# The last four chunks of a gathered adjacency: rows written straight to their place

## The chip, the cores and the metric

The kernel runs on one core of a Trainium2 chip. The time is device time in microseconds of one execution, as a median of runs. "Before" is the kernel that was tuned already, "after" the same kernel with one change.

## The reference

The input x has the shape (8, 2048, 128), adj is 2048 x 2048 with some 0.4% of entries that are not zero, its diagonal among them. All is float32. B = 8 batches are stacked side by side, so that a row of 128 nodes times (8 x 128) numbers is a chunk; there are 16 chunks.

```python
# layer 0
res = si[:, :, None] + sj[:, None, :] + relation[None] * w_r + g_b     # relation = adj
agg = einsum('bij,bjd->bid', res, inputs)
x   = layernorm(x + agg @ weight + bias)
# layer 1 (both matrices are adj)
x1  = einsum('bnf,nw->bwf', x, A)
x2  = 2.0 * einsum('bnf,nw->bwf', x1, A) - x
x   = layernorm(x + relu(concat(x, x1, x2, x1, x2) @ Theta1 + bias))
```

So adj is multiplied in three times: once as it is in layer 0, and twice transposed in layer 1, which the kernel does as two hops, the first from u to y, the second from y to the output.

## The kernel before

**Sparse rows.** For a block of columns of adj only the rows with an entry count. The kernel finds them on the chip and writes lists of row numbers. Each of the 16 column chunks of 128 has 7 lists of up to 128 rows: four "T" lists, one for each 32 columns; two, one for each 64 columns; and one for the whole 128. The last three are called "H". A product with adj is then, for each chunk, 7 gathers of rows of the right factor (4 KB each, up to 128 rows, into tile `Y` by an indirect DMA) and matmuls of these with the same rows of adj, 32, 64 or 128 columns wide, that were kept in `rc` (for the hops) and `rct` (for layer 0), and one product with the chunk's own 128 x 128 block, whose block of adj (`rd`) and rows are loaded by SP.

**Dense chunks.** In layer 0 the first ND = 4 chunks are computed with all rows. So they need no entry in `rct`; their rows in `rc` are needed in hop 1, where they come as the 11th to 14th of 16 chunks, and in hop 2.

**Filling rc and rct.** A list of `jobs` fills them. A job is one chunk's T lists (4 gathers) or H lists (3 gathers): `get_job` issues the gathers into a staging place, `keep_job` later multiplies by `has`, which is 0 where a list has no row, on DVE, and writes `rc` and `rct`. The 24 jobs of chunks 4 to 15 gather pieces of 256 numbers from `rr_d`, into four places in `st`. The 8 jobs of the dense chunks gather pieces of 128 numbers from adj by the indices `idr`, each of 128 columns of which 32, 64 or 128 are used, and have one staging place, `trp[:, 2]`. So each of these waits for the DVE instructions of the one before it.

**Stages.** Up to some 150 us adj is read and transposed, x is multiplied by the weight, and chunks 0 and 1 of layer 0 are summed. From 150 to 205 us DVE makes the second set of lists (`lists_end` writes the row numbers `idx` and the piece numbers `idr`, which are row times pieces per row plus `col`) while jobs begin. Chunks 2 and 3 of layer 0 follow, dense. From 261 us the loop over chunks c = 4 to 15 of layer 0 runs: rows of the next chunk (`get_rows`), a `keep_job`, a `get_job`, own rows, `rank9`, the listed rows T and H, `z_add`, `make_u` of an earlier chunk (which writes u_d), the load of x two chunks ahead, and `layernorm`. Hop 1 runs from some 432 us, hop 2 from 625.

**Order.** Every engine runs its queue in order. POOL issues all gathers, SP the loads, ACT the stores of u_d, y_d and the output. Rows go into 12 places of `Y` in turn, so a gather waits until PE has used the twelfth one before it. A scheduler places instructions that have nothing to wait for earlier than the text has them; the four gathers of the first dense job, for one, stand in the list stage.

The lines that the change replaces in the loops of layer 0 and of hop 1:

```python
        if c < 15:
            keep_job()
        if c < 13 or c == 14:
            get_job()
...
            if i == 1 and (k % 2 and k < 12 or k == 12):
                keep_job()
                if k < 12:
                    get_job()
```

All times of instructions stand under line 72 in the profile, a helper that records them; so they are told apart by their tiles.

Of the kernel before, what the change touches and what calls it, by code (L numbers as in the profile page):

```python
# [11 lines left out]
ALU = mybir.AluOpType  # L12
# [6 lines left out]
def kernel(  # L19
# [22 lines left out]
    P = 128  # L42
    B, N, D = x.shape
    NC = N // P
    HB = B // 2
    BD = B * D
    TW = 32
    NT = N // TW
    QT = P // TW
    ND = 4  # L50
# [3 lines left out]
    HC = NT // 2 + NC  # L54
    NI = NT + HC
    PAD = 40000
    W = 3 * P
# [16 lines left out]
    pe, dve, act = Tied(nc.tensor), Tied(nc.vector), Tied(nc.scalar)  # L74
    pool, sp = Tied(nc.gpsimd), Tied(nc.sync)

    y0_d = nc.dram_tensor("y0_d", (N, BD), F32).ap()
    rr_d = [nc.dram_tensor(f"rr_d{c}", (N, 2, P), F32).ap() for c in range(ND, NC)]
# [67 lines left out]
    num = const.tile([P, NC], F32)  # L146
    dve.tensor_copy(num, numi)
    coli = const.tile([P, NI], I32)
    pool.iota(coli[:, 0:NT], pattern=[[1, NC], [0, QT]], base=0, channel_multiplier=0)
    pool.iota(coli[:, NT:NT + 2 * NC], pattern=[[1, NC], [0, 2]], base=0, channel_multiplier=0)  # L150
    pool.iota(coli[:, NT + 2 * NC:], pattern=[[1, NC]], base=0, channel_multiplier=0)
    col = const.tile([P, NI], F32)
    dve.tensor_copy(col, coli)
# [41 lines left out]
    zs = {}  # L195
# [126 lines left out]
    def acc_pair():  # L322
        par[0] ^= 1
        return bank[2 * par[0]:2 * par[0] + 2]
# [143 lines left out]
    def lists_end(part):  # L468
        b = bank[6 + part]
        if part == 0:  # L470
            lo, hi = 0, NT
            for r in range(2):
                pe.matmul(
                    b[64 * r:64 * r + 64, 0:NT], lists, ident[:, 64 * r:64 * r + 64], start=True,
                    stop=True, skip_group_check=True, tile_position=(0, 64 * r),
                )
        else:
            lo, hi = NT, NI
            for r in range(2):
                pe.matmul(  # L480
                    b[64 * r:64 * r + 64, 0:HC], lists2[0:2 * HC],
                    ident[0:2 * HC, r * HC:(r + 1) * HC], start=True, stop=True,
                    skip_group_check=True, tile_position=(0, 64 * r),
                )
        pl = b[:, 0:hi - lo]
        s = slice(lo, hi)
        rown = small.tile([P, NT], F32, name=f"rown{part}", tag="rown")[:, 0:hi - lo]
        dve.tensor_scalar(has[:, s], pl, 0.0, None, op0=ALU.is_gt)
        dve.tensor_scalar(rown, pl, 0.0, float(PAD + 1), op0=ALU.is_equal, op1=ALU.mult)
        dve.scalar_tensor_tensor(rown, pl, -1.0, rown, op0=ALU.add, op1=ALU.add)  # L490
        dve.tensor_copy(idx[:, s], rown)
        dve.scalar_tensor_tensor(rown, rown, float(NC), col[:, s], op0=ALU.mult, op1=ALU.add)
        dve.tensor_copy(idr[:, s], rown)
        if part:
            dve.tensor_reduce(miss[:, 2:3], has, AX.X, ALU.add)
            dve.tensor_sub(miss[:, 0:1], miss[:, 0:1], miss[:, 1:2])
            dve.tensor_sub(miss[:, 0:1], miss[:, 0:1], miss[:, 2:3])

    def overflow():
# [3 lines left out]
            b[0:1, 0:1], miss[:, 0:1], ones[:, 0:1], start=True, stop=True, skip_group_check=True,  # L503
        )
        dve.tensor_scalar(over, b[0:1, 0:1], 0.5, None, op0=ALU.is_gt)

    adj128 = adj.rearrange("n (c f) -> (n c) f", f=P)

    def gather(to, src, ids, n, rows):
        pool.indirect_dma_start(  # L510
            out=to, out_offset=None, in_=src,
            in_offset=bass.IndirectOffsetOnAxis(ap=ids[:, n:n + 1], axis=0),
            bounds_check=rows - 1, oob_is_err=False,
        )
# [6 lines left out]
    def strided(t, n, step, w):  # L521
        return t[:, 0:n * step].rearrange("p (n s) -> p n s", s=step)[:, :, 0:w]

    jobs = [("T", c) for c in T_ORDER] + [("H", c) for c in range(ND, NC)]
    for c in range(ND):
        jobs += [("T", c), ("H", c)]
    got, kept = [0], [0]
    last = trp[:, 2].rearrange("p i f -> p (i f)")

    def staged(k):  # L530
        return st[:, k % 4 * BD:] if jobs[k][1] >= ND else last

    def get_job():
        what, c = jobs[got[0]]
        s = staged(got[0])
        got[0] += 1
        for n, i in enumerate(columns(c, what)):
            if c >= ND:
                gather(
                    s[:, n * 2 * P:(n + 1) * 2 * P], rr_d[c - ND].rearrange("n m f -> n (m f)"), idx,  # L540
                    i, N,
                )
            else:
                gather(s[:, n * P:(n + 1) * P], adj128, idr, i, N * NC)

    def keep_job():
        what, c = jobs[kept[0]]
        s = staged(kept[0])
        kept[0] += 1
        m = 2 if c >= ND else 1  # L550
        hc = has[:, columns(c, what)[0]:columns(c, what)[0] + QT]
        for k in range(m):
            if m == 1 or k == 1:
                to = rc[:, c * W:(c + 1) * W]
            else:
                to = rct[:, (c - ND) * W:(c - ND + 1) * W]
            of = s[:, k * P:]
            if what == "T":
                if m == 2:
                    dve.tensor_mul(  # L560
                        to[:, 0:P].rearrange("p (t f) -> p t f", t=QT),
                        strided(of, QT, m * P + TW, TW), hc[:, :, None].to_broadcast([P, QT, TW]),
                    )
                    continue
                for t in range(QT):
                    at = t * (P + TW)
                    dve.tensor_scalar(
                        to[:, TW * t:TW * t + TW], of[:, at:at + TW], hc[:, t:t + 1], None,
                        op0=ALU.mult,
                    )  # L570
                continue
            step = m * P + 64
            dve.tensor_mul(
                to[:, P:2 * P].rearrange("p (t f) -> p t f", t=2), strided(of, 2, step, 64),
                hc[:, 0:2, None].to_broadcast([P, 2, 64]),
            )
            i = NT + 2 * NC + c
            dve.tensor_scalar(
                to[:, 2 * P:3 * P], of[:, 2 * m * P:2 * m * P + P], has[:, i:i + 1], None,
                op0=ALU.mult,  # L580
            )

    def make_ub():
        cs = [trp[:, h].rearrange("p i f -> p (i f)") for h in range(2)]
# [42 lines left out]
    def layernorm(z, name):  # L627
        s = small.tile([P, 4, B], F32, name=f"s_{name}", tag="s")
        dve.tensor_reduce(s[:, 0], z, AX.X, ALU.add)
        dve.tensor_scalar(s[:, 1], s[:, 0], 1.0 / D, None, op0=ALU.mult)  # L630
        dve.tensor_sub(z, z, s[:, 1][:, :, None].to_broadcast([P, B, D]))
        for h in range(2):
            hs_ = slice(h * HB, (h + 1) * HB)
            sq = small.tile([P, HB, D], F32, name=f"sq_{name}_{h}", tag="sq", bufs=1)
            act.activation(sq, z[:, hs_, :], AF.Square)
            dve.tensor_reduce(s[:, 2, hs_], sq, AX.X, ALU.add)
        act.activation(s[:, 3], s[:, 2], AF.Sqrt, bias=epst, scale=1.0 / D)
        rs = small.tile([P, B], F32, name=f"rs_{name}", tag="rs")
        dve.reciprocal(rs, s[:, 3])
        dve.tensor_mul(z, z, rs[:, :, None].to_broadcast([P, B, D]))  # L640

    atx = at4.rearrange("p c (k b f) -> p (c k) b f", k=2, b=B)
    x1t = [atx[:, c] for c in range(8)] + [Y[:, c] for c in range(4, 8)]
# [195 lines left out]
    for c in range(ND, NC):  # L839
        if c > ND:  # L840
            if c > ND + 1:
                get_rows(0, c, "T", y0_d)
            get_rows(0, c, "H", y0_d)
        if c < 15:
            keep_job()
        if c < 13 or c == 14:
            get_job()
        accs = acc_pair()
        own_rows(0, c, accs, True)
        if c + 2 < NC:  # L850
            own0(c + 2)
        rank9(c, accs)
        if c + 1 < NC:
            si_t(c + 1)
        listed(0, c, accs, "T")
        listed(0, c, accs, "H")
        z_add(accs, zs[c])
        for n in [c - 2] if c < 14 else [12, 13] if c == 14 else [14]:
            make_u(n, zs[n], x1t[n], u_of[n])
        if c + 2 < NC:  # L860
            load_z(c + 2)
        layernorm(zs[c], f"0_{c}")


    def hop(i, src, order, there, between):
# [51 lines left out]
        for k, c in enumerate(order):  # L917
            rows(k, "H")
            if k > 1:
                begin(k)  # L920
            fetch(k + 2)
            if k > 0:
                rows(k + 1, "T")
            if i == 1 and (k % 2 and k < 12 or k == 12):
                keep_job()
                if k < 12:
                    get_job()
            listed(i, c, accs[k], "H")
            end(c, accs[k])

# [1 line left out]
        1, u_d, list(range(ND, 14)) + list(range(ND)) + [14, 15], range(12, NC),  # L932
        lambda: make_u(NC - 1, zs[NC - 1], x1t[NC - 1], u_of[NC - 1]),
    )
    assert kept[0] == len(jobs)
    homes[4:9] = homes[9:14]
    hop(
        2, y_d, list(range(9, 14)) + list(range(ND)) + [14, 15] + list(range(4, 9)),
# [96 lines left out]
```

## Time and profile before

| what | value |
|---|---|
| median of 3 runs | 808.93 us (806.57 to 810.0) |
| the profiled execution | 818.08 us, its span 816.3 us, mean granted clock 0.971 |
| busy: PE, DVE, ACT, POOL | 732.8, 394.7, 192.7, 445.2 us |
| gathers of Y from y0_d and y_d ("y_d" in the profile) | 196, mean 1081 ns on POOL |
| gathers of Y from u_d | 112, mean 999 ns |
| gathers into st from rr_d | 84, mean 1075 ns |
| gathers of adj into trp | 28, mean 1010 ns, 5.8 us from issue to landing |

The profile is of one execution. POOL's time of a gather is what it takes to issue it; the transfer follows on the DMA engines. "Idle before" in a timeline is how long the engine had been idle before an instruction, and what ended that. The DMA share of a window is the mean busy share of 16 DMA engines, and GB/s what they moved. A waiting PE is later charged to what landed last.

### The profile page before, as it was taken

Reading aid. Unit: us, or ns where it says so; the run is one execution under the profiler, and the core shown is the slowest. Engines: PE = TensorE matmul, PEld = TensorE weight load, DVE = VectorE, ACT = ScalarE, POOL = GpSimd, SP = SyncE. Lnnn points to the kernel's source line nnn. Section 1 sums busy time; section 2 is a strip of 40 time slices with the busy share of each in tenths; the row PEclk is TensorE's granted clock in tenths of the full one; section 3 lists DMA queues with packets and bytes.
Section 4 is the critical chain, followed back from the end, with each engine's and each line's share of the span. In section 5 each row is a group of like instructions: output and inputs, shape, how many; then the busy total and the mean of one; then the engine's idle time right before and its main releaser. Section 6 shows DMA issues by size and latency. Waiting matters only on the chain.

```text
span 816.3 us, 10067 instructions
## 1 busy us (share of the span) xinstructions
PE 732.8 (90%) x3554; PEld 364.9 (45%) x3554; DVE 394.7 (48%) x591; ACT 192.7 (24%) x439; POOL 445.2 (55%) x432
## 2 busy tenths in 40 slices
PE   4999999997999998988798888898899999999992
PEld 4666566642644343434345243333344454444441
DVE  4664876578341655555533000000100377777775
ACT  3757554321200332313222000000000011111101
POOL 1000000477747876776344677776774777776740
PEclk9999999997999999999899899999999999999997
DMA  8999999999326799999969799899999799999982
GB/s 264 296 314 316 352 292 295 314 398 347 119 89 223 244 346 368 341 344 367 356 224 344 246 364 360 314 365 346 339 372 357 252 343 357 370 385 389 363 299 68
DMA packets 165299, 253.90 MB, mean 311 GB/s; under 512 B 17255, under 2 KB 118020, under 8 KB 163192
## 3 DMA queue, kind: packets, MB, share of 16 engines
q0 software_dynamic: 49280, 146.52, 49.7%
q1 hardware_dynamic: 93200, 81.01, 31.1%
q10 hardware_dynamic: 22760, 25.63, 8.9%
q8 instruction: 30, 0.49, 0.2%
q14 instruction: 29, 0.24, 0.1%
HBM read 234.82 MB, written 58.72 MB: 360 GB/s over the span
## 4 chain that ended last, share of the span: by engine, by line
PE 52%; DMA 29%; issue 6%; ACT 6%; DVE 3%; POOL 2%; ACTq 0%; POOLq 0%; SPq 0%; DVEq 0%
PE bank L72 52%; DMA Y<-u_d,idx 12%; DMA Y<-y_d,idx 8%; DMA st<-rr_d,idx 2%; DMA rd<-rr_d 2%; ACT Y L72 2%; DMA ring<-in_x_dram 2%; POOL Y L72 1%; ACT rct L72 1%; ACT trp L72 1%; DMA trp<-in_adj_dram,idr 1%; DVE s L72 1%; DVE ring L72 1%; ACT at L72 1%; DVE st L72 1%
## 5 line engine op out<-in xcount | busy, mean ns | idle before, releaser
L72 POOL DMA_INDIRECT Y<-y_d,idx x196 | 212.0, 1081 | 93.2 <-PE bank L72 38.0
L72 PE MATMUL bank<-Y,rc 128*32 128x512 f32 (+2 forms) x896 | 219.7, 618 | 21.3 <-DMA Y<-u_d,idx 19.1
L72 POOL DMA_INDIRECT st<-rr_d,idx x84 | 90.3, 1075 | 183.5 <-DVE rown L72 148.3
L72 POOL DMA_INDIRECT Y<-u_d,idx x112 | 111.8, 999 | 53.9 <-issue 29.9
L72 PEld LDWEIGHTS bank<-Y,rc 128*32 128x32 f32 (+2 forms) x896 | 58.6, 130 | 179.3 <-issue 99.5
L72 PE MATMUL bank<-Y,at 128*128 128x512 f32 x256 | 115.2, 601 | 0.0
L72 PE MATMUL bank<-Y,rct 128*32 128x512 f32 (+2 forms) x336 | 77.3, 625 | 8.5 <-DMA Y<-y_d,idx 8.5
L72 DVE TENSOR_REDUCE s<-sq 128x4 f32<-128x512 f32 x64 | 43.9, 686 | 58.0 <-ACT sq L72 58.0
L72 PEld LDWEIGHTS bank<-Y,at 128*128 128x128 f32 x256 | 47.8, 193 | 53.6 <-issue 53.4
L72 DVE COPY ring<-bank 128x512 f32<-128x512 f32 x10 | 6.9, 692 | 110.1 <-PE bank L72 110.1
L72 ACT ACTIVATE sq<-ring 128x512 f32<-128x512 f32 x44 | 27.7, 630 | 129.5 <-DVE ring L72 109.7
L72 PE MATMUL bank<-ring,rd 128*128 128x512 f32 x108 | 51.5, 599 | 5.7 <-DMA rd<-rr_d 4.1
L72 PE MATMUL bank<-ident,rc 128*128 128x128 f32 (+2 forms) x302 | 45.0, 297 | 12.6 <-DMA rc<-in_adj_dram 6.6
L72 PE MATMUL bank<-th,at 128*128 128x128 f32 x384 | 49.2, 283 | 1.9 <-ACT at L72 1.9
L72 PEld LDWEIGHTS bank<-th,at 128*128 128x128 f32 x384 | 46.8, 197 | 6.7 <-ACT at L72 3.8
L72 DVE TENSOR_TENSOR ring<-bank,ring 128x512 f32<-128x512 f32 x26 | 17.3, 688 | 66.0 <-PE bank L72 60.8
L72 DVE TENSOR_REDUCE st<-rc 128x64 f32<-128x2048 f32 x16 | 36.5, 2283 | 25.7 <-DMA rc<-in_adj_dram 25.7
L72 ACT COPY ring<-bank 128x512 f32<-128x512 f32 x34 | 19.9, 586 | 122.5 <-PE bank L72 112.9
L72 PEld LDWEIGHTS bank<-Y,rct 128*32 128x32 f32 (+2 forms) x336 | 20.8, 130 | 57.3 <-issue 32.4
L72 PEld LDWEIGHTS bank<-ident,rc 128*128 128x128 f32 (+2 forms) x302 | 33.8, 150 | 25.5 <-issue 9.1
L72 PE MATMUL bank<-wx,trp 128*128 128x130 f32 x256 | 36.9, 288 | 4.3 <-ACT trp L72 2.2
L72 PE MATMUL bank<-ident,ring 128*128 128x128 f32 x232 | 32.5, 282 | 6.4 <-DMA ring<-in_x_dram 2.8
(142 smaller groups left out, 789.1 us busy)
## 6 DMA issues: line engine op xcount, KB each, us to landing
rc<-in_adj_dram SPq DMA_DIRECT2D x16, 1024.0 KB, 10.9
ring<-in_x_dram SPq DMA_DIRECT2D x25, 512.0 KB, 8.5
rr_d<-in_adj_dram SPq DMA_DIRECT2D x12, 1024.0 KB, 10.8
rr_d<-Y SPq DMA_DIRECT2D x8, 1024.0 KB, 9.0
y_d<-Y SPq DMA_DIRECT2D x16, 512.0 KB, 10.6
u_d<-ring ACTq DMA_DIRECT2D x12, 512.0 KB, 7.0
ring<-y_d SPq DMA_DIRECT2D x11, 512.0 KB, 23.2
ring<-u_d SPq DMA_DIRECT2D x10, 512.0 KB, 3.9
```

Source lines behind the costliest of these rows:

```text
L72: return lambda *a, **k: tc.keep_in_program_order(f(*a, **k))
```

## The change

The dense chunks have no jobs any more. Their 28 gathers write straight into `rc`, each piece just as wide as its list's columns (32, 64 or 128 numbers), so `idr` counts pieces of that width. A gather leaves rows without an entry untouched; so `rc` of a dense chunk is first set to zero, by a comparison "below 0" of a number that the layernorm of chunk 8, 11, 12 or 14 has just computed and that is never below 0. Of the gathers 22 are written in the loop of layer 0 at chunks 10 to 15, and 6 in hop 1, one for each of its first chunks. The tile `trp[:, 2]` is no longer used for staging, and the 24 DVE instructions that masked the dense rows are gone.

```diff
-    pool.iota(coli[:, 0:NT], pattern=[[1, NC], [0, QT]], base=0, channel_multiplier=0)
-    pool.iota(coli[:, NT:NT + 2 * NC], pattern=[[1, NC], [0, 2]], base=0, channel_multiplier=0)
+    pool.iota(coli[:, 0:NT], pattern=[[1, NT]], base=0, channel_multiplier=0)
+    pool.iota(coli[:, NT:NT + 2 * NC], pattern=[[1, 2 * NC]], base=0, channel_multiplier=0)
...
-        dve.scalar_tensor_tensor(rown, rown, float(NC), col[:, s], op0=ALU.mult, op1=ALU.add)
+        for a, z, m in ((0, 32, 32), (32, HC, NC)) if part else ((0, NT, NT),):
+            dve.scalar_tensor_tensor(
+                rown[:, a:z], rown[:, a:z], float(m), col[:, lo + a:lo + z], op0=ALU.mult,
+                op1=ALU.add,
+            )
...
-    for c in range(ND):
-        jobs += [("T", c), ("H", c)]
...
+    direct = []
+    for c in range(ND):
+        direct += [(c * W + t * TW, TW, QT * c + t) for t in range(QT)]
+        direct += [(c * W + P + t * 64, 64, NT + 2 * c + t) for t in range(2)]
+        direct += [(c * W + 2 * P, P, NT + 2 * NC + c)]
+
+    def clear(c, rs):
+
+        dve.tensor_scalar(
+            rc[:, c * W:(c + 1) * W], rs[:, 0:1].to_broadcast([P, W]), 0.0, None, op0=ALU.is_lt
+        )
+
+    def get_direct(n):
+        for at, w, i in direct[:n]:
+            gather(
+                rc[:, at:at + w], adj.rearrange("n (c f) -> (n c) f", f=w), idr, i, N * (N // w)
+            )
+        del direct[:n]
...
-        if c < 15:
+        if kept[0] < len(jobs):
             keep_job()
-        if c < 13 or c == 14:
+        if got[0] < len(jobs):
             get_job()
+        get_direct({10: 2, 11: 3, 12: 4, 13: 4, 14: 5, 15: 4}.get(c, 0))
...
-        layernorm(zs[c], f"0_{c}")
+        rs = layernorm(zs[c], f"0_{c}")
+        if c in (8, 11, 12, 14):
+            clear((8, 11, 12, 14).index(c), rs)
...
-            if i == 1 and (k % 2 and k < 12 or k == 12):
-                keep_job()
-                if k < 12:
-                    get_job()
+            if i == 1:
+                get_direct(1)
```

`layernorm` now returns `rs`, the reciprocal of the standard deviation.

More of the change, by code (lines that the diff above doesn't have):

```diff
@@ L505, in overflow @@
         dve.tensor_scalar(over, b[0:1, 0:1], 0.5, None, op0=ALU.is_gt)
-    adj128 = adj.rearrange("n (c f) -> (n c) f", f=P)
     def gather(to, src, ids, n, rows):
@@ L524 @@
     jobs = [("T", c) for c in T_ORDER] + [("H", c) for c in range(ND, NC)]
-    for c in range(ND):
-        jobs += [("T", c), ("H", c)]
     got, kept = [0], [0]
-    last = trp[:, 2].rearrange("p i f -> p (i f)")
     def staged(k):
-        return st[:, k % 4 * BD:] if jobs[k][1] >= ND else last
+        return st[:, k % 4 * BD:]
     def get_job():
@@ L537, in get_job @@
         for n, i in enumerate(columns(c, what)):
[L538 to L544, printed above, removed]
+            gather(
+                s[:, n * 2 * P:(n + 1) * 2 * P], rr_d[c - ND].rearrange("n m f -> n (m f)"), idx, i,
+                N,
+            )
     def keep_job():
@@ L549, in keep_job @@
         kept[0] += 1
-        m = 2 if c >= ND else 1
         hc = has[:, columns(c, what)[0]:columns(c, what)[0] + QT]
[L552 to L556, printed above, removed]
+        for k in range(2):
+            to = rc[:, c * W:(c + 1) * W] if k else rct[:, (c - ND) * W:(c - ND + 1) * W]
             of = s[:, k * P:]
             if what == "T":
[L559 to L570, printed above, removed]
+                dve.tensor_mul(
+                    to[:, 0:P].rearrange("p (t f) -> p t f", t=QT), strided(of, QT, 2 * P + TW, TW),
+                    hc[:, :, None].to_broadcast([P, QT, TW]),
+                )
                 continue
-            step = m * P + 64
             dve.tensor_mul(
-                to[:, P:2 * P].rearrange("p (t f) -> p t f", t=2), strided(of, 2, step, 64),
+                to[:, P:2 * P].rearrange("p (t f) -> p t f", t=2), strided(of, 2, 2 * P + 64, 64),
                 hc[:, 0:2, None].to_broadcast([P, 2, 64]),
@@ L578, in keep_job @@
             dve.tensor_scalar(
-                to[:, 2 * P:3 * P], of[:, 2 * m * P:2 * m * P + P], has[:, i:i + 1], None,
-                op0=ALU.mult,
-            )
+                to[:, 2 * P:3 * P], of[:, 4 * P:5 * P], has[:, i:i + 1], None, op0=ALU.mult
+            )
+    direct = []
[6 more added lines that the diff above has]
+            rc[:, c * W:(c + 1) * W], rs[:, 0:1].to_broadcast([P, W]), 0.0, None, op0=ALU.is_lt
+        )
+    def get_direct(n):
+        for at, w, i in direct[:n]:
+            gather(
+                rc[:, at:at + w], adj.rearrange("n (c f) -> (n c) f", f=w), idr, i, N * (N // w)
+            )
+        del direct[:n]
     def make_ub():
@@ L640, in layernorm @@
         dve.tensor_mul(z, z, rs[:, :, None].to_broadcast([P, B, D]))
+        return rs
     atx = at4.rearrange("p c (k b f) -> p (c k) b f", k=2, b=B)
@@ L934 @@
     )
-    assert kept[0] == len(jobs)
+    assert kept[0] == len(jobs) and not direct
     homes[4:9] = homes[9:14]
```

## The prediction

> **What bounds the kernel now.** I read the chain of work that ended last first, then the windows by stage, then the timelines of POOL, PE and SP in the two stages that the change touches.
>
> ```profile
> PE 52%; DMA 29%; issue 6%; ACT 6%; DVE 3%; POOL 2%; ACTq 0%; POOLq 0%; SPq 0%; DVEq 0%
> PE bank L72 52%; DMA Y<-u_d,idx 12%; DMA Y<-y_d,idx 8%; DMA st<-rr_d,idx 2%; DMA rd<-rr_d 2%; ACT Y L72 2%; DMA ring<-in_x_dram 2%; POOL Y L72 1%; ACT rct L72 1%; ACT trp L72 1%; DMA trp<-in_adj_dram,idr 1%; DVE s L72 1%; DVE ring L72 1%; ACT at L72 1%; DVE st L72 1%
> ```
>
> Half of the chain is matmul; the largest other piece, 12%, is gathers of u_d, that is hop 1. The windows (columns as in their heading) show what that stage lacks.
>
> ```profile
> core 0: us, PE busy (x) PEld busy (x) DVE busy (x) ACT busy (x) POOL busy (x), PEclk, DMA share, GB/s
> 340.00:376.00 36.00, 33.44 (x168) 14.96 (x165) 20.98 (x35) 11.70 (x24) 27.19 (x28) 1.00 0.99 344
> 376.00:410.00 34.00, 26.72 (x121) 11.33 (x120) 15.55 (x30) 8.13 (x16) 13.85 (x14) 0.90 1.00 363
> 447.00:613.00 166.00, 146.81 (x649) 58.82 (x645) 13.17 (x34) 8.21 (x14) 120.28 (x122) 0.95 0.93 337
> 590.00:613.00 23.00, 21.84 (x103) 9.07 (x103) 1.39 (x2) 1.17 (x2) 16.54 (x18) 0.93 1.00 373
> ```
>
> In 447 to 613 POOL issues 122 gathers, each 0.99 us and then 0.30 us of issue: one per 1.295 us, 158 us of the 166. In 590 to 613, where none of them is a small gather of adj, the transfers run at 373 GB/s; over the whole stage at 337. So hop 1 is bound by POOL's issue rate, with transfers close behind. The reason stands in POOL's timeline:
>
> ```profile
> 456.49 0.99 POOL L72 DMA_INDIRECT Y<-u_d,idx  x1 [0.30 <-issue]
> 460.76 1.00 POOL L72 DMA_INDIRECT trp<-in_adj_dram,idr  x1 [3.29 <-DVE rc L72]
> 462.06 1.00 POOL L72 DMA_INDIRECT trp<-in_adj_dram,idr  x1 [0.30 <-issue]
> 463.37 0.99 POOL L72 DMA_INDIRECT trp<-in_adj_dram,idr  x1 [0.30 <-issue]
> 464.67 0.99 POOL L72 DMA_INDIRECT Y<-u_d,idx  x1 [0.30 <-issue]
> ```
>
> A 64 KB gather of adj holds POOL as long as a 512 KB gather of Y, and the first of a group also waits 3.29 us for DVE to empty the one staging place. PE's floor in hop 1 is lower: the begin of a chunk stands at 596.49 and of the next at 605.63 when nothing is missing, 9.14 us, against a mean of (614.77 - 463.18)/13 = 11.7 us.
>
> In layer 0 PE waits too, but not always for POOL:
>
> ```profile
> 363.36 3.85 PE L72 MATMUL bank<-Y,rct 128*64 128x512 f32 x10 [1.44 <-DMA Y<-y_d,idx]
> 377.33 3.84 PE L72 MATMUL bank<-Y,rct 128*64 128x512 f32 x10 [1.10 <-DMA Y<-y_d,idx]
> 402.08 2.49 PE L72 MATMUL bank<-ring,rd 128*128 128x512 f32 x4 [4.07 <-DMA rd<-rr_d]
> 382.54 1.18 SPq L72 DMA_DIRECT2D rd<-rr_d  x1
> 410.68 0.99 POOL L72 DMA_INDIRECT Y<-y_d,idx  x1 [10.61 <-PE bank L72]
> 425.39 0.99 POOL L72 DMA_INDIRECT Y<-u_d,idx  x1 [6.88 <-issue]
> ```
>
> In chunks 11 and 12 it waits for gathers, POOL being busy without a break until 376. In chunk 14 it waits for its own block, issued on SP at 382.54 and landed at 402.08. POOL by then has gaps (4.46 us before 391.32, 10.61 before 410.68, 6.88 before 425.39; some 23 us with smaller ones).
>
> **The change, part by part.** The instruction order of the two built programs tells where the 28 gathers of adj stand. Before: 4 in the list stage (172.96 to 178), 4 at 412 to 417, 20 between the u_d gathers from 460.76 on. After: 2 ahead of chunk 11's rows, 3 ahead of chunk 12's, 16 between there and the first u_d gather, 7 among the first ten u_d gathers and before the H rows of hop 1. None is later.
>
> *Hop 1.* 20 gathers and the wait go from 447 to 613: 20 x 1.295 + 3.0 = 29 us of POOL, which would leave 137 us. Transfers are next. The stage moved 337 x 166 = 55.9 MB, of which the 20 small ones were at most 20 x 64 KB = 1.3 MB; 54.6 MB at the 373 GB/s of the stretch without them is 146 us, at 360 GB/s 152. I take 151, since gathers will still be held by buffers now and then: -15 us (-29 if POOL alone ruled, -6 if only the transfer time of the 20 goes: their packets at the mean of the ACT queue q10, whose 8.9% of 16 engines' span are 1162 us for 22760 packets, 0.05 us, are 128 x 0.05/16 = 0.4 us each). PE's floor, 9.14 us a chunk, lies below all of these.
>
> *Layer 0, POOL.* The 5 gathers ahead of the rows of chunks 11 and 12 delay these by 2.6 and 6.5 us, and both chunks already wait: up to 6.5 us. Later ones, 16 - 4 = 12 more, 15.6 us, fit into the 23 us of gaps, since rows of chunks 13 to 15 lie some 6, 10 and 20 us ahead of PE. The delay is not all kept: chunk 13 waits 1.64 us and chunk 14 4.07 us for loads whose issue follows the own rows of two chunks earlier (about 30 us from those to landing). With PE 6.5 us late, chunk 13's wait goes (4.9 left), and chunk 14's load, shifted by chunk 11's 2.6, leaves about 2.5 us. After the 4.07 us gap the four own matmuls took 2.49 us instead of 1.88, the rows 7.33 instead of 5.71, at a granted clock of 0.78 in 395 to 410; a shorter gap may save some of that. Against it stands transfer time: the share is 1.00 there, and 12 more small gathers at 0.4 us are 5 us. I take +3 (-2 to +9).
>
> *Start of hop 1.* 7 gathers stand among the first u_d gathers. Two push T rows of the first chunks by 1.3 us each; five fall into the gap before 447.43, where POOL waited 6.85 us for the last u_d to land. They take 6.5 us, so without that cover they would cost 6.5; I take +1.
>
> *DVE.* The 24 masking instructions of the dense chunks go (16 x 0.24, 4 x 0.29, 4 x 0.285, 5 us): nothing, DVE is busy 13 of 166 us in hop 1, and the one POOL wait for them is counted. Four clears of 128x384 come: no such row; between 0.28 (128x128) and 0.69 us (128x512), nearer to the latter, 0.55 each. They follow layernorms 8, 11, 12 and 14, ahead of gaps of 2 to 5 us: nothing; at worst 2.2. One instruction is added to the second list step, on DVE's chain near 192.6: +0.2.
>
> *List stage.* 4 gathers leave POOL at 173 to 178. Nothing: POOL then stops 8.79 us before 234.74 for DVE, and that gap only grows.
>
> *Clears as a wait.* A small gather at the head of POOL's queue now waits for a layernorm, with the next rows behind it. Layernorms 11, 12 and 14 end at 375.95, 390.58 and 426.66; with shifts of 2.6 and 4.9 us in the first two and 0.55 us for the clear that is 379, 396 and, plus the last shift, 427. POOL reaches the places at about 373.3 + 9.1 = 382, after 400, and at 428 plus the last shift. Margins of 3, 4 and 1 us: nothing, but the last is thin, and u_d gathers queue behind it.
>
> Sum: -15 + 3 + 1 + 0.2, about -11. The profiled execution took 818.08 us, 1.8 more than its span of 816.3; it would take 807. It lay 9.15 above the median of 808.93, so the median goes to 798.
>
> **A rule weighed.** The change makes pieces of 512 bytes into pieces of 128 (16 gathers) and 256 (8). The row nearest to a small packet is the ACT queue's 0.05 us at 1.1 KB, which as a bound gives the 0.4 us above. The Trainium skill, "DMA: Bandwidth & Descriptors", Specifications, says that below 512 bytes a transfer loses line rate since it becomes a read-modify-write: a rule against this change. If that doubled a packet, the 12 extra gathers would cost 10 us instead of 5, and the sum would be -6. No run shown so far settles it.
>
> **Rivals.**
> *Gain hidden.* Hop 1 keeps its DMA-bound time (share 0.93: 154 busy us, less 6 for the small ones, with the same holes), so it gives 8, and layer 0 pays the whole 6.5. For it: the share is above 0.9 throughout. Against: 373 GB/s in 590 to 613 with POOL at full pace. Time: 818 - 8 + 8, no change, 807.
> *All of POOL's time.* Hop 1 gains 24 and layer 0 pays nothing, its later waits eating the delay: 808.9 - 23 = 786. Against: a chunk moves 4 MB (7 gathers of some 0.43 MB, by the 35.7 MB and 70 gathers of hop 2's window 640 to 740 at 357 GB/s less 0.59 MB a chunk of other loads and stores; own rows and store of 0.52 MB each), 10.8 us at 373 GB/s and not 9.1.
> *Slower: small packets in the full stage.* From 340 to 410 the transfers have no room. If a 128- or 256-byte packet took as long as a 4 KB one in the saturated stretch (4096 B at 373/16 GB/s, 0.18 us), a gather would cost 1.4 us, the 17 extra ones 24 us ahead of hop 1, and chunks 12 to 15 would wait for own loads; hop 1 gives 15: 809 + 9 = 818. It decides from about 0.11 us a packet on (17 x 128 x 0.11/16 = 15). Against: the 0.05 us row.
> *Not what it says.* The gathers could be moved early, as 4 were before; the instruction order excludes it.
>
> **How the numbers follow.** Forecast 0.58 (798, itself 791 to 804), hidden 0.18 (804 to 811), all 0.12 (784 to 791), slower 0.12 (811 to 822). The range from 787 to 809 leaves out the ends. Differences within 0.5% (4 us, 804.9 to 813.0) count as none, about what a measurement of this kernel can tell. Faster: 0.58 + 0.12 + a little of hidden = 0.72; same 0.16; slower 0.12.
>
> **What would show it.** Right: no adj gather after the H rows of hop 1 begin; 102 gathers of u_d there in about 150 us at above 360 GB/s; chunk 12's wait for gathers up by 4 us, chunk 14's wait for its load down. Wrong: the stage from the first H row of hop 1 shorter by less than 8 us; PE waiting over 5 us in chunk 14 or 15; POOL waiting for DVE at one of the clears, with u_d rows behind.

## The result: 0.4% slower, and where the time went

The changed kernel takes 813.93 us (median; 811.64 to 816.64), beside 809.93 us (806.57 to 817.54) for the kernel before: a ratio of 1.0038, 95% interval 1.002 to 1.0056. The forecast was 798 us.

The chain of work that ended last, in the profile of the changed kernel:

```profile
PE 48%; DMA 32%; issue 6%; ACT 6%; DVE 3%; POOL 3%; ACTq 0%; POOLq 0%; DVEq 0%
PE bank L72 48%; DMA Y<-u_d,idx 15%; DMA Y<-y_d,idx 13%; DMA st<-rr_d,idx 3%; ACT Y L72 2%; POOL Y L72 2%; DMA ring<-in_x_dram 1%; ACT rct L72 1%; ACT trp L72 1%; DVE lists L72 1%; ACT at L72 1%; DVE s L72 1%; DVE st L72 1%; DVE ring L72 1%; DMA gb<-in_L_gnn_g_b_dram 1%
```

The gathers of y_d, which are layer 0's here (and later hop 2's), have gone from 8% to 13% of it. The windows of the changed kernel show the two stages:

```profile
core 0: us, PE busy (x) PEld busy (x) DVE busy (x) ACT busy (x) POOL busy (x), PEclk, DMA share, GB/s
340.00:376.00 36.00, 32.57 (x152) 14.32 (x153) 19.11 (x32) 11.05 (x23) 27.80 (x27) 1.00 0.89 303
376.00:410.00 34.00, 28.53 (x136) 11.62 (x134) 17.25 (x30) 7.99 (x17) 25.12 (x26) 0.90 0.93 323
447.00:613.00 166.00, 153.37 (x706) 65.52 (x706) 10.37 (x15) 9.40 (x17) 108.75 (x111) 0.98 0.96 356
590.00:613.00 23.00, 22.50 (x109) 10.07 (x108) 1.38 (x2) 1.17 (x2) 15.38 (x17) 1.00 0.98 362
```

In hop 1 POOL has idle time now, 111 gathers in place of 122, and the transfers move 356 GB/s. From 376 to 410 it is the other way round: POOL is busy 25.12 of 34 us where it was busy 13.85 before (21.00 in before_a, told next), and the transfers fell from 363 to 323 GB/s (from 340 to 376, from 344 to 303). Another execution of the kernel before (called before_a below), 10 us shorter than the one that the prediction read, has this window:

```profile
447.00:613.00 166.00, 150.65 (x688) 62.40 (x688) 13.86 (x35) 8.79 (x15) 123.38 (x125) 0.99 0.96 351
```

351 GB/s at a share of 0.96, and not 337 at 0.93. So hop 1 had less to win than it seemed: 351 to 356.

Three marks tell the stages apart in every profile: the own rows of hop 1's first chunk ("k0") on PE, its first 64-wide listed matmul ("H", the one behind the last u_d), and the group of 16 theta matmuls with which hop 2 begins. The rows below the fourth are of experiments told further down. All are in us from the start of the span; "hop 1" is the last mark less H. These are profiles from chips on which the kernel before takes 810 to 811 us.

| profile | chunk 12 | 13 | 14 | 15 | k0 | H | theta of hop 2 | hop 1 |
|---|---|---|---|---|---|---|---|---|
| before, as predicted from | 370.20 | 385.97 | 402.08 | 420.91 | 434.27 | 451.66 | 625.16 | 173.5 |
| before_a | 368.87 | 382.55 | 396.42 | 412.01 | 425.38 | 446.80 | 616.58 | 169.8 |
| before_b | 368.21 | 382.09 | 395.63 | 411.95 | 425.38 | 446.19 | 617.66 | 171.5 |
| after | 371.69 | 392.41 | 404.22 | 423.05 | 436.41 | 458.25 | 620.37 | 162.1 |
| none | 370.06 | 383.95 | 397.03 | 412.54 | 425.90 | 447.38 | 612.09 | 164.7 |
| first5_c | 372.74 | 389.98 | 401.78 | 417.30 | 430.67 | 451.90 | 618.28 | 166.4 |
| not_first_c | 370.83 | 384.86 | 399.86 | 417.69 | 431.23 | 457.14 | 618.93 | 161.8 |
| late_c | 369.28 | 382.88 | 396.28 | 411.80 | 425.16 | 449.63 | 616.34 | 166.7 |
| gap | 370.82 | 384.50 | 396.90 | 412.42 | 425.79 | 447.51 | 615.38 | 167.9 |
| gap2 | 369.37 | 383.78 | 398.90 | 417.73 | 431.09 | 452.51 | 615.30 | 162.8 |
| no_own_c | 373.95 | 392.36 | 404.17 | 424.90 | 438.27 | 459.64 | 611.86 | 152.2 |

Against the mean of before_a and before_b, the changed kernel reaches H 11.8 us later, runs hop 1 in 8.5 us less (162.1 against 170.6), and so begins hop 2 3.3 us later; hop 2 takes as long as before (190.1 us from the mark to the end of the span, beside 189.9). That fits the 4.0 us between the medians. The marks are of single executions, which differ by 1 to 2 us: chunk 12, for one, stands at 368.21 to 370.83 in the versions without gathers of adj among the rows of chunks 11 and 12.

Where do the 11.8 us come from? POOL's timeline of the changed kernel, with lines left out:

```profile
376.02 1.00 POOL L72 DMA_INDIRECT rc<-in_adj_dram,idr  x1 [0.30 <-DMA Y<-y_d,idx]
...
382.47 0.98 POOL L72 DMA_INDIRECT Y<-y_d,idx  x1 [1.54 <-DMA Y<-y_d,idx]
...
391.56 1.00 POOL L72 DMA_INDIRECT rc<-in_adj_dram,idr  x1 [0.30 <-issue]
...
421.03 0.99 POOL L72 DMA_INDIRECT Y<-y_d,idx  x1 [0.30 <-issue]
...
430.13 1.00 POOL L72 DMA_INDIRECT Y<-u_d,idx  x1 [4.20 <-PE bank L72]
```

Between 340 and 430 POOL issues every 1.3 us, with two gaps only. The line at 421.03 is the last gather of layer 0, a row of chunk 15. In before_a, where the gaps are, the same gather stands at 406.98:

```profile
387.82 1.33 POOL L72 DMA_INDIRECT Y<-y_d,idx  x1 [2.19 <-PE bank L72]
...
401.77 1.00 POOL L72 DMA_INDIRECT Y<-y_d,idx  x1 [2.75 <-PE bank L72]
...
406.98 1.00 POOL L72 DMA_INDIRECT Y<-y_d,idx  x1 [0.31 <-issue]
...
420.19 0.99 POOL L72 DMA_INDIRECT Y<-u_d,idx  x1 [10.91 <-PE bank L72]
...
442.55 0.99 POOL L72 DMA_INDIRECT Y<-u_d,idx  x1 [6.79 <-DMA u_d<-st]
```

From 340 to that last row before_a has eight gaps of 0.48 us or more, 8.9 us together, which is 6.5 beyond the usual 0.30 us of issue. Its two large gaps, 10.91 and 6.79 us, lie behind the row. The changed kernel puts 18 gathers of adj ahead of it, where before_a has three: 15 more, 15 x 1.295 = 19.4 us. The gaps can take 6.5 of them, 12.9 are left, and the row is 14.05 us later. The lead that POOL had over PE covers a part; PE waits for the rest:

```profile
381.77 7.64 PE L72 MATMUL bank<-Y,rct 128*32 128x512 f32 x22 [4.93 <-DMA Y<-y_d,idx]
411.47 1.93 PE L72 MATMUL bank<-Y,rct 128*64 128x512 f32 x6 [1.10 <-DMA Y<-y_d,idx]
```

The first is in chunk 12, the second in chunk 14. By chunks the lag of after behind before_a is 2.8 us at chunk 12, 9.9 at 13, 7.8 at 14, 11.0 at 15 and 11.0 at k0: chunk 12 loses 7, chunk 13 wins 2 back, chunk 14 loses 3. The wait of 4.93 us is not all of chunk 12's loss: the 22 matmuls behind it took 7.64 us, where all 28 of chunk 13 took 5.71 at a granted clock of 1.00 (395.51 us). From 382 to 388 us the granted clock was 0.68, and by these numbers it cost some 3 us (an estimate).

### The profile page after: what moved, and what is told of

It is laid out like the page before. It is cut to its first block, busy times and chain, and to the rows that moved or that the text cites. A ratio compares the mean times of both kernels' runs of the same rounds, so it can differ in the third digit from the quotient of the medians.

```text
span 810.5 us, 10025 instructions
## 1 busy us (share of the span) xinstructions
PE 730.5 (90%) x3554; PEld 363.8 (45%) x3554; DVE 391.5 (48%) x572; ACT 192.2 (24%) x439; POOL 446.0 (55%) x432
## 2 busy tenths in 40 slices
DMA packets 165299, 252.96 MB, mean 312 GB/s; under 512 B 17256, under 2 KB 118333, under 8 KB 163192
## 4 chain that ended last, share of the span: by engine, by line
PE 48%; DMA 32%; issue 6%; ACT 6%; DVE 3%; POOL 3%; ACTq 0%; POOLq 0%; DVEq 0%
PE bank L72 48%; DMA Y<-u_d,idx 15%; DMA Y<-y_d,idx 13%; DMA st<-rr_d,idx 3%; ACT Y L72 2%; POOL Y L72 2%; DMA ring<-in_x_dram 1%; ACT rct L72 1%; ACT trp L72 1%; DVE lists L72 1%; ACT at L72 1%; DVE s L72 1%; DVE st L72 1%; DVE ring L72 1%; DMA gb<-in_L_gnn_g_b_dram 1%
## 5 line engine op out<-in xcount | busy, mean ns | idle before, releaser
L72 PE MATMUL bank<-Y,rc 128*32 128x512 f32 (+2 forms) x896 | 216.3, 612 | 17.1 <-DMA Y<-u_d,idx 14.6
L72 PE MATMUL bank<-Y,rct 128*32 128x512 f32 (+2 forms) x336 | 80.9, 619 | 15.2 <-DMA Y<-y_d,idx 15.2
L72 ACT COPY Y<-bank 128x256 f32<-128x256 f32 (+1 forms) x72 | 27.8, 397 | 44.0 <-PE bank L72 43.7
```

The costliest lines, as they stand in the source:

```text
L72: return lambda *a, **k: tc.keep_in_program_order(f(*a, **k))
```

## The experiments

The ratio is always to the kernel before on the same chip. The first comparison, the fourth and the fifth were on chips on which the kernel before takes 811 us. The second and the third fell on two other chips, on which it takes 849 and 850 us, at a lower clock and with pauses in layer 0 that the first ones do not have; of these, called the slower chips, the ratios are told, and no stage of theirs is compared with another chip's.

**The kernel before, twice more (before_a, before_b).** No edit.

> The kernel before, unchanged, for a second profile: the first was taken in an execution of 818.08 us, 8 above the median of 22 runs (809.93). Theory Q (POOL's queue: the moved gathers stand ahead of layer 0 rows for which POOL has no slack in a usual run): a usual execution of 808 to 811 us in which chunk 14 does not wait 4 us for its own block, the low clock of 395 to 410 us is missing, and the first H matmul of hop 1 stands at 442 to 446 us instead of 451.66, so that layer 0 really got 12 to 16 us later and hop 1 got 11 us shorter. Theory P (small packets of 128 and 256 bytes load the DMA engines in layer 0): the same here. Theory U (the profile of before was usual up to hop 1, and the 8 us lie elsewhere): first H matmul again at 451 to 452 us, and the difference in hop 1 or hop 2.

> The kernel before, a third profile. Q and P: 806 to 812 us, first H matmul of hop 1 at 442 to 446 us; U: 451 to 452.

808.29 and 809.26 us. Both reach k0 at 425.38 us, 8.9 us earlier than the profile of the prediction, and run hop 1 2 to 3.7 us faster. In that profile PE had waited 4.07 us for an own block in chunk 14, at a clock of 0.78; here the only such waits are 1.84 us in chunk 14 of before_a and 0.56 us in chunk 15 of before_b.

**Without the 28 gathers (none).**

```diff
-        for at, w, i in direct[:n]:
-            gather(...)
         del direct[:n]
```

> The kernel after without the 28 gathers of adj for the dense chunks (their rows in rc stay zero, so their part of layer 1 is left out); clears and all else stay. It is the floor for every placement of the 28. Q: the 21 that stand ahead of hop 1 cost up to 21 x 1.3 = 27 us there, less what gaps cover: 797 to 803 us. P: the packets alone cost the difference to before, 795 to 803. If neither holds (the loss comes from the clears or from the staging place being gone): 810 to 814.

802.47 us, ratio 0.9865 (0.9814 to 0.9916). Beside the changed kernel's 1.0038 that is 14 us, the cost of all 28 gathers where the change has them. Against the kernel before the whole removal gains 11 us (4 us either way), and hop 1 becomes only 5.9 us shorter (170.6 to 164.7). The profiles show 6 of the 11, since before_a and before_b lie 2 to 3 us below their chip's median of 811.12; where the rest is they do not tell. Its window of hop 1, columns as above:

```profile
447.00:613.00 166.00, 157.78 (x705) 65.24 (x706) 11.04 (x16) 9.36 (x16) 105.66 (x107) 0.98 0.97 358
```

With not one gather of adj left the transfers stand at 0.97 and 358 GB/s. The forecast's 151 us for 166, 15 less, was more than there was to be had.

**The same gathers with their rows out of range (oob).**

```diff
-        for a, z, m in ((0, 32, 32), (32, HC, NC)) if part else ((0, NT, NT),):
+        for a, z, m in ((0, 32, 8192), (32, HC, 8192)) if part else ((0, NT, 8192),):
```

> The kernel after with the pieces' row numbers multiplied by 8192 for 64, 32 and 16, so that nearly all rows of the 28 gathers lie out of range and move nothing: POOL issues the same gathers at the same places, and the packets are gone (the dense chunks' part of layer 1 is left out). Q: 811 to 815 us, as after, since POOL's issue is what costs. P: 797 to 804, near the kernel without the gathers.

815.41 us, ratio 1.0043 (1.0017 to 1.0069), as the changed kernel; H at 458.82 us, hop 1 of 163.0. The counts of the trace, first of the changed kernel, then of this one:

```profile
DMA packets 165299, 252.96 MB, mean 312 GB/s; under 512 B 17256, under 2 KB 118333, under 8 KB 163192
```

```profile
DMA packets 165299, 252.36 MB, mean 311 GB/s; under 512 B 17693, under 2 KB 118455, under 8 KB 163192
```

0.60 MB are gone, yet the number of packets is the same. The kernel before, and none, for comparison:

```profile
DMA packets 165299, 253.90 MB, mean 311 GB/s; under 512 B 17255, under 2 KB 118020, under 8 KB 163192
```

```profile
DMA packets 164401, 252.32 MB, mean 315 GB/s; under 512 B 16798, under 2 KB 117559, under 8 KB 162296
```

none has 898 fewer, 896 of them on POOL's queue, which is 32 for each of the 28 gathers. So a gather of 128 pieces shows as 32 packets, and it keeps them when nearly all of its rows are out of range. The bytes of the small pieces show no price, and the loss of layer 0 stays without them. That a packet as such costs nothing is not shown by this run, though it was meant to; what speaks on it is that the versions below keep the same pieces, in other places, and no longer show the loss.

**Seven behind the rows of chunk 15, seven behind the ninth u_d gather, fourteen in hop 1 (late, late_b, late_c).** The clears move with them; those in hop 1 read a number of the y that its chunk has just made, times 0.

```diff
-        get_direct({10: 2, 11: 3, 12: 4, 13: 4, 14: 5, 15: 4}.get(c, 0))
+        get_direct({15: 7}.get(c, 0))
...
-        if c in (8, 11, 12, 14):
-            clear((8, 11, 12, 14).index(c), rs)
+        if c in {13: 0, 15: 1}:
+            clear({13: 0, 15: 1}[c], rs)
...
-                get_direct(1)
+                get_direct({0: 7, 3: 2, 4: 2, 5: 2, 6: 2, 7: 2, 8: 2, 9: 2}.get(k, 0))
...
+            if i == 1 and k in {2: 2, 5: 3}:
+                clear({2: 2, 5: 3}[k], flat(homes[c])[:, BD - 1:BD])
```

> The gathers written straight to rc, but none ahead of any row of layer 0: 7 behind the last rows of chunk 15, where POOL stands still some 10 us for u_d, 7 after the 9th gather of u_d, where it stands still some 7 us for the last u_d, and 14 in hop 1, two for each of seven chunks, held there by clears that read results of hop 1. Theory Q (POOL's issue, charged where POOL has no slack): layer 0 as before, first H matmul of hop 1 at 446 to 449 us, hop 1 shorter by 2 to 6 us than before, together 804 to 809 us where before has 810. Theory Z (writing straight to rc, the clears or the missing staging cost by themselves): first H matmul later than 452, no gain.

0.989 (0.9844 to 0.9937), on the first of the slower chips. Repeated on the other:

> The version with 7 of the 28 gathers behind the rows of chunk 15, 7 behind the ninth u_d gather and 14 in hop 1, two per chunk from its fourth on, again. Theory (placement decides): ratio 0.985 to 0.993, first matmul of hop 1 within 5 us of the kernel before, hop 1 shorter by at least 4 us. Rival (its earlier gain was the other chip's): 0.997 to 1.006, as the changed kernel.

0.9832 (0.977 to 0.9893). And on a chip like the first:

> The version with 7 of the 28 gathers behind the rows of chunk 15, 7 behind the ninth u_d gather and 14 in hop 1, a third time, for a chip on which the kernel before takes about 810 us. Theory (placement decides): ratio 0.985 to 0.993 there, that is 798 to 804 us; first matmul of hop 1 at 446 to 452 us, hop 1 of 162 to 166 us. Rival (the gain was that of a chip on which the kernel before takes 849 us): above 0.997.

808.35 us, ratio 0.9965 (0.9943 to 0.9987). So it is below both kernels, all three times; the size is 0.35% on the last chip and 1.1 and 1.7% on the slower ones, and why it is larger there is open. On the last chip the ratio lies outside of the expected 0.985 to 0.993. POOL's timeline shows the place:

```profile
403.20 0.99 POOL L72 DMA_INDIRECT Y<-y_d,idx  x1 [0.30 <-PE bank L72]
...
420.02 1.00 POOL L72 DMA_INDIRECT Y<-u_d,idx  x1 [5.87 <-PE bank L72]
```

The last row of layer 0 is issued at 403.20, the seven gathers of adj take the time behind it, and the first u_d gather still waits 5.87 us for a place in `Y`. k0 stands at 425.16, as in the kernel before.

**Seven behind layer 0's rows, 21 in hop 1 in groups of four and three (straight).** The seven stand as in the late version, and the clears move along:

```diff
-                get_direct(1)
+                get_direct({1: 4, 3: 3, 5: 4, 7: 3, 9: 4, 11: 3}.get(k, 0))
```

> The gathers written straight to rc, at about the old places: 7 behind the last rows of layer 0, then groups of 4 and 3 among the u_d gathers of hop 1, 21 in all as before (20). What is left of the change is that there is no staging, no masking on DVE and no wait of POOL for it (1.7, 4.0 and 3.3 us in three profiles of before). Q: before less 0 to 4 us, 806 to 810. Z: 812 or more.

1.0024 (0.9983 to 1.0065), on a slower chip: no gain to be seen. 21 in hop 1 are about as many as the kernel before has there.

**Both kernels again, on a slower chip (before_c, after_b).**

> The kernel before, profiled beside the three that follow. Ratio 1 by every theory. On a chip like that of the first comparison: first matmul of hop 1 at 446 to 447 us from the span's start, hop 1 of 170 to 172 us, POOL waiting for PE about 10 us near 410 us and 7 us at the u_d gathers, and not 23 us in all as in the first profile; on a chip with a clock near 0.95 all of these later.

852.47 us, k0 at 440.63 us, with a pause of 11 us on ACT in layer 0.

> The changed kernel once more, on the same chip as the next two. Theory (the 21 gathers ahead of the first u_d gather cost layer 0 about as much as hop 1 gains): ratio 1.002 to 1.006, first matmul of hop 1 10 to 13 us later than in the kernel before, hop 1 shorter by 7 to 9 us. Rival (the first result was a matter of the chip): a ratio under 0.997.

1.0006 (0.9964 to 1.0048): the interval holds the first result, and no difference too.

**Only the five early ones back (first5, first5_c).** Beside the late version, the gathers ahead of the rows of chunks 11 and 12, with the clear of the first dense chunk back at chunk 8:

```diff
-        get_direct({15: 7}.get(c, 0))
+        get_direct({10: 2, 11: 3, 15: 2}.get(c, 0))
```

> The version before this one, with one thing changed: five of the seven gathers that stood behind the rows of chunk 15 stand where the change has them, two ahead of the rows of chunk 11 and three ahead of those of chunk 12; the clear of the first dense chunk moves with them to the layernorm of chunk 8. Theory, by the prediction's term of up to 6.5 us for these five: 3 to 7 us above the version before, ratio near 0.995. Rival (the later gathers of chunks 12 to 15 cost the time, the first five are eaten by later waits): within 2 us of the version before.

0.9977 (0.9934 to 1.0019) against 0.9832 of the late version beside it, some 11 to 12 us, uncertain by 6. On the chip like the first:

> The same version with five of its gathers ahead of the rows of chunks 11 and 12. Theory, by the prediction's term for the five: 3 to 7 us above the version before this one, chunk 12 waiting for its gathers about 5 us. Rival (later waits eat the delay of the five): within 2 us of it.

812.88 us, ratio 1.003 (1.0008 to 1.0053), 4.5 us above late_c, as the theory expected; k0 is 5.5 us later (430.67 against 425.16). Later waits do not eat the delay of the five. The wait itself is shorter than expected, 2.31 us in chunk 12 and not 5. The rest lies in waits in chunk 11 and in slower matmuls: the ten behind chunk 12's wait took 5.49 us, where ten in the profile of the prediction took 3.84, and the granted clock was 0.73 from 382 to 388.

**Only the later ones (not_first, not_first_c).** 21 still ahead of the first u_d gather, but none ahead of the rows of chunk 12:

```diff
-        get_direct({10: 2, 11: 3, 12: 4, 13: 4, 14: 5, 15: 4}.get(c, 0))
+        get_direct({12: 4, 13: 4, 14: 5, 15: 4}.get(c, 0))
...
-                get_direct(1)
+                get_direct(6 if k == 0 else 1)
```

> The kernel after, but the 5 gathers ahead of the rows of chunks 11 and 12 moved behind those of chunk 12; still 21 ahead of hop 1. Q, as I put it in the prediction (only those 5 hurt, later ones fit into gaps): first H matmul at 447 to 450 us, 802 to 806 us. Q with the whole queue (POOL has some 16 us of gaps ahead of hop 1 and gets 22 us of issue): still 4 to 9 us later than before, 808 to 813 us.

0.9961 (0.9915 to 1.0007), on a slower chip. Again:

> The change with the five gathers moved behind the rows of chunk 12, 21 of the 28 still ahead of the first u_d gather. If the five alone carried layer 0's loss: first matmul of hop 1 at 447 to 452 us and 5 to 8 us less than the changed kernel's 814. If the 16 later ones carry as much: at 452 to 456 us and 2 to 4 us less.

809.96 us, ratio 0.9979 (0.9959 to 0.9998), 4 to 5 us less than the changed kernel, by medians and by ratios. k0 stands at 431.23, 6.1 us later than in late_c. So both halves cost: 5.5 us at k0 for the five, 6.1 for the later ones, 11.6 together, beside 11.3 in the changed kernel (436.41 less 425.16). That they add up so well is partly luck, since of the 6.1 us 1.6 stand already at chunk 12 (370.83 against 369.28), ahead of whose rows this version has no gather of adj. H came at 457.14, later than either expectation, since the gathers that were moved now stand ahead of the H rows of hop 1.

**Without the loads of the own rows in hop 1 (no_own, no_own_c).**

```diff
-                load_own(i, src, order[k], homes[order[k]], order[k] in there)
+                load_own(i, src, order[k], homes[order[k]], i == 1 or order[k] in there)
```

> The kernel after without the loads of own rows in hop 1 (12 x 512 KB; the own product then takes what lies in the place, so this part of hop 1 is left out). Tells what holds hop 1 now that POOL has gaps in it. Transfers: hop 1, 162 us from the first H matmul to the start of hop 2, gets 10 to 14 us shorter, 799 to 804 us. Buffers, latency or PE: less than 4 us shorter, 810 or more.

0.9956 (0.9917 to 0.9996), on a slower chip. Again:

> The changed kernel without the loads of the own rows in hop 1 (12 of 512 KB, 6.3 MB of its 57 MB), again: its own products there read what lies in their places. Theory (after the change the transfers hold hop 1): hop 1 of 147 to 156 us against 162, 6 to 15 us less than the changed kernel's 814. Rival (POOL, or PE's waits for places, hold it): 160 us or more, within 3 us.

804.33 us, ratio 0.9915 (0.9888 to 0.9943): some 10 us less than the changed kernel. Hop 1 falls from 162.1 to 152.2 us with POOL's work unchanged. Its window of hop 1:

```profile
447.00:613.00 166.00, 158.05 (x759) 69.88 (x760) 11.08 (x16) 10.95 (x19) 114.73 (x117) 0.98 0.95 351
```

So after the change hop 1 is held by its transfers: taking 6.3 MB away, 17.7 us at 356 GB/s, gives 9.9 us. Why not more is not shown; PE, busy 158 of the window's 166 us, is probably next.

**Into POOL's wait ahead of layer 0's loop (gap).** Near 230 us POOL waits 10.1 us for DVE and the DMA share is 0.2. Beside the late version:

```diff
-    layernorm(zs[1], "0_1")
+    clear(0, layernorm(zs[1], "0_1"))
...
     next_job()
+    get_direct(7)
     layernorm(zs[2], "0_2")
...
-        if c in {13: 0, 15: 1}:
-            clear({13: 0, 15: 1}[c], rs)
+        if c == 13:
+            clear(1, rs)
...
-                get_direct({0: 7, 3: 2, 4: 2, 5: 2, 6: 2, 7: 2, 8: 2, 9: 2}.get(k, 0))
+                get_direct({3: 2, 4: 2, 5: 2, 6: 2, 7: 2, 8: 2, 9: 2}.get(k, 0))
```

> The late version, but the seven gathers of the first dense chunk stand among the last gathers into st ahead of chunk 4, where POOL of the changed kernel waits 10 us for DVE near 230 us and the DMA share is 0.2; the clear of that chunk reads the layernorm of chunk 1. Chunk 1's seven stand behind the rows of chunk 15, the other 14 in hop 1 as in the late version; none is left behind the ninth u_d gather. Theory (only a place where POOL truly idles is free, each other one pays 1.3 us in part): 2 to 6 us below the late version's 808, ratio 0.988 to 0.995, first matmul of hop 1 at 445 to 449 us. Rival (the places of the late version cost nothing either, hop 1 is held by transfers): 806 to 810, ratio above 0.995.

808.32 us, ratio 0.9964 (0.994 to 0.9989): as the late version, so the theory fell here. H came 2.1 us earlier than in late_c, and hop 1 took 1.2 us longer.

**And seven fewer in hop 1 (gap2).** The clears move along:

```diff
-                get_direct({3: 2, 4: 2, 5: 2, 6: 2, 7: 2, 8: 2, 9: 2}.get(k, 0))
+                get_direct({0: 7, 4: 2, 6: 2, 8: 2, 10: 1}.get(k, 0))
```

> As gap, but with chunk 2's seven behind the ninth u_d gather, so that only seven are left in hop 1. Theory (hop 1 held by its transfers): the seven fewer in hop 1 give at most 2 us, the seven ahead of the H rows cost 0 to 4: 0 to 4 us above gap. Rival (POOL still holds hop 1): 4 us or more below gap.

808.07 us, ratio 0.9949 (0.9917 to 0.998), as gap: H 5.0 us later, hop 1 5.1 us shorter. This is the lowest of the versions that compute everything, though not apart from late_c and gap by their intervals. late_c, gap and gap2 begin hop 2 at 616.34, 615.38 and 615.30 us, whatever H does. So a later H seems to make hop 1, as it is measured here, shorter by itself.

## Why the prediction was wrong

Two terms of the sum failed, by about as much: hop 1 gave 6.5 us less than forecast, and layer 0 cost 8 us more.

**What bounds the kernel.** Half right. POOL's rate did hold hop 1, with transfers close behind, but closer than read: the profile was of an execution 9 us above the median, with 337 GB/s in hop 1 where 347 (before_b) and 351 (before_a) are usual.

**Hop 1, -15.** The term was mis-sized; it measured -8.5, and part of that may be the later H alone, since none has -5.9. From 349, the mean of before_a and before_b, to 356 GB/s are 2%; the 20 gathers of adj, 1.3 MB at most (20 x 64 KB), are 2% of some 58 MB; 4% of 170.6 us are 7 us (an estimate). The prediction took 361 GB/s, near the rate of the last 23 us, against 337. What 590 to 613 moves, 362 also after the change, is not what a whole stage moves. none, with -5.9, and no_own_c say the same: the transfers hold it.

**Layer 0, +3, and the start of hop 1, +1.** Layer 0 is the step whose mechanism failed: k0 comes 11.0 us later in place of 3. From k0 to H it is 0.7 us more, so the +1 was right. The prediction set the 12 later gathers, 15.6 us, against "23 us of gaps", and so at nothing. Of these gaps 6.88 us stood behind the last row of layer 0, where no gather ahead of that row could use them. The 10.61 us stood ahead of its last two rows, as POOL's timeline of that profile shows:

```profile
410.68 0.99 POOL L72 DMA_INDIRECT Y<-y_d,idx  x1 [10.61 <-PE bank L72]
...
415.88 1.00 POOL L72 DMA_INDIRECT Y<-y_d,idx  x1 [0.30 <-issue]
```

But they belong to that one execution, in which POOL waited there for a PE that was itself late (4.07 us for its own block, at a clock of 0.78). From 340 us to the last row that profile has 17.2 us of gaps beyond the 0.30 us of issue, before_a 6.5 and before_b 7.2; in these two the large gap, 10.91 and 10.28 us, stands behind the row. So a usual execution had room for some five of the gathers. Rows that lie 6, 10 and 20 us ahead of PE did not save it: with POOL's gaps used up this lead went too, and the last row of layer 0 came 14 us later. not_first_c gives up to 6.1 us at k0 for what was costed at nothing.

The five ahead of the rows of chunks 11 and 12 were rightly costed at up to 6.5 us: chunk 12's wait of 4.93 us is there, and first5_c shows 5.5 us. But the prediction let waits for own loads in chunks 13 and 14 eat half of it. The 4.07 us were of that one execution; against before_a only some 2 us come back, between the marks of chunks 13 and 14, where before_a waits 1.84 us for chunk 14's own block. And the lower clock that followed the wait in chunk 12 was not in the sum, though the prediction had read 0.78 behind such a wait.

**DVE, clears, list stage.** Right, as far as the trace shows. The four clears:

```profile
L72 DVE TENSOR_SCALAR rc<-rs x4: 353/362/390, 332.9 to 428.7; 128x384 f32<-128x384 f32 x4
```

They take 0.36 us (0.55 was the estimate), and no gather waits for one. POOL waits 10.10 us for DVE in the list stage, where it had waited 8.79.

**The rule weighed.** The Trainium skill, "DMA: Bandwidth & Descriptors", Specifications, speaks against pieces under 512 bytes. No run here shows a price for it: without 0.60 MB of those pieces oob takes as long, and late_c has all of them and is some 6 us below the changed kernel. Nor does the trace show the pieces singly: it counts 32 packets for a gather and not the 128 of the prediction's 0.4 us, which by its 0.05 us a packet would be 0.1 us (an estimate), and as many under 512 B before the change as after (17255 and 17256). So the rule was not put to the test. The packets alone were not taken away, so their price is bounded and not measured: in late_c all 28 gathers, POOL's part and packets together, cost 1% or 8 us beside none, 0.3 us each.

**The rivals.** "Gain hidden" was the nearest: hop 1 gave the 8 us that it said, and layer 0 paid more than its 6.5. (Its sum, 818 - 8 + 8 less 9, is 809 and not 807, and 20 gathers at 0.4 us are 8 us and not the 6 that the prediction has twice.) "All of POOL's time" falls with none and no_own_c. "Small packets in the full stage" had a range that holds 814, but its mechanism isn't what happened: in that stage the transfers have room after the change, 303 and 323 GB/s in the windows above, and it is POOL's issue that has none. What the runs showed in its place is a slower case that the prediction did not have: small gathers ahead of rows, each 1.3 us of POOL, with the gaps on the wrong side of these rows.

**What stays open.** The 28 gathers are 36 us of POOL, and the best placing found costs some 7 us beside none; which part of the end of hop 1 pays them isn't settled. Nor is the larger gain of the late version on the slower chips.

## What to carry to other kernels

Gaps of a queue are worth something only to work that can be issued in them: add up the idle time between the place of the new instruction and the first instruction that someone waits for, and nothing behind it. An engine whose gaps are all its lead over its consumer isn't idle. And a profile 1% above its median should be set against a second one before its longest waits and gaps are used as cover.

## What was unexpected in the hardware

A gather whose 128 rows are nearly all out of range costs POOL as much as one that moves them (1006 ns in oob, 1003 in the changed kernel), and the trace counts as many packets: 165299 in both.

The kernel before took 811 us on three chips and 849 to 850 on two others; the mean granted clock was 0.975 in before_b and 0.953 in before_c. On the slower ones long pauses stand in layer 0: 11 us in before_c, and 23 us in late, where the same copy waits 7.62 us a chunk earlier. The line of ACT in the profile of late (start, length, instruction, idle time before it):

```profile
367.19 1.07 ACT L72 COPY at<-bank 128x512 f32<-128x512 f32 x2 [23.19 <-remote]
```

What ACT waited for the trace does not tell.
